# A graph-network kernel's prelude: the edge list on 124 partitions with four blocks each, places counted by two engines, ranks before most node tables, edge lists masked at their first use

## The chip, the cores and the metric

The kernel runs on one core of one Trainium2 chip. The metric is the device time of one execution in microseconds (us), the median of several runs; lower is better. A core has five engines that work through instruction queues of their own: TensorE (PE in the profile; its weight loads are PEld), VectorE (DVE), ScalarE (ACT), GpSimd (POOL) and SyncE (SP). Transfers are started from the queues of SP and ACT, and, where the addresses come out of a tile in on-chip memory, from POOL ("indirect" gathers and scatters).

## The reference

The reference is two layers of a graph transformer on 3125 nodes of 256 features, with 103125 directed edges sorted by their destination (`dst`), each with a source (`src`) and one of eight types.

```python
xn = _layernorm(x)
x = x + _L0_gnn_ref(xn, src, dst, ...) + _L0_mix_ref(xn, ...)     # max over the edges of a node
x = x + _L0_ffn_ref(_layernorm(x), ...)                          # experts chosen for the whole graph
xn = _layernorm(x)
x = x + _L1_gnn_ref(xn, src, dst, edge_type_8, ...) + _L1_mix_ref(xn, ...)   # sum over the edges of a node
x = x + _L1_ffn_ref(_layernorm(x), ...)                          # two of eight experts for each node
```

In layer 0 the graph part of node n is `relu(theta(x_n - x_s) + phi(x_s))`, maximised over all edges s to n. As the part of n is constant, the kernel maximises rows of a table `btab` = normalised x times (phi - theta), and adds the node's own part afterwards. In layer 1 it is a sum of rows picked from a table by source and type.

## The kernel before

**Layout.** 3125 nodes are 25 tiles of 128. Nearly all arithmetic is float32. The node tile t=24 has 53 real rows.

**The prelude** (lines 922 to 1230) turns the sorted edge list into a form in which one indirect gather brings one edge for each of 128 nodes:

1. *Places.* For each node its place `en` is needed, the number of edges whose destination is at most that node. It is found in two steps. `firsts` holds the first destination of each block of 128 edges (806 blocks), read by a transfer of single numbers into `blk0`, turned round by seven products on PE and copied by ACT (L1097, L1098). A quad is four tiles in which partition p holds nodes 4p to 4p+3; there are seven quads, the last with one tile. For each quad `counts_of` (DVE, L1057) or `signs_of` (ACT, L1050) counts the blocks that begin at or below the quad's first node, `stretches_of` fetches a stretch of 416 destinations for each partition from there (POOL, `row`), and `places_of` (DVE, L1076) counts in it for each of the quad's tiles. `at_i` is the place as an integer.
2. *Lists.* `edges_of` (POOL, `raw`) fetches for every node the 64 entries of the combined index `e_idx` (source times 8 plus type) that end at its place; those that belong to other nodes are to be masked. There are 25 such fetches.
3. *Degrees and ranks.* `dg` is the difference of neighbouring places. Nodes are ranked by falling degree, by a one-hot `hot` of 66 degree keys, products on PE (L1146), copies on ACT (L1147), a scan and a sum on DVE (L1178 to L1184). The result is `in_i`, the node that stands at each rank, made by 25 one-hot products (L1225, L1226).
4. *Tables.* `node_stats` (DVE) and `node_table` (ACT, PE) normalise x and make `btab`, five tiles at a time (`fives`). `ntab` holds for each node its x and its list: x is copied early by five transfers, `masks(g)` (DVE, L1160 to L1162, three operations a quad) replaces foreign entries by a padding index and writes the lists.
5. *Checks.* `bad` (L1169 to L1175) is a test of whether the edge list is sorted and has the loops that the fast form needs; a general form of the kernel exists for other inputs and isn't taken here.

**Layer 0** follows in `fast()`: `fetch` gathers `nrow`, the rows of `ntab` in order of rank (POOL, `ask`), and splits them into x and the indices `idx1`, `idx2` (DVE, L1497, L1502). Then `edge_pass` makes for tile t `STEPS[t]` gathers of 128 rows of `btab`, at most four in one buffer, maximised on DVE. Because ranks fall in degree, a tile needs only as many gathers as its largest node has edges (814 in all). Dense work (attention, experts) is interleaved with these from a list with costs. `outputs_out` copies a product into a spare buffer `y1` (`SECONDS` of them) until `outputs_b` adds it on DVE.

**What sets the order.** In the prelude the queues of DVE, POOL and PE follow the program text (`manual_schedule`); ACT's and SP's are arranged by a planner. The first two fetches of layer 0 stand outside such a region, so there the planner arranges DVE too. Each queue is worked through in order: an instruction that waits holds all behind it. Transfers use eight completion counters in turn, so each new transfer of SP or ACT first waits for the one eight before it.

Of the kernel before, what the change touches and what calls it, by code (L numbers as in the profile page):

```python
# [20 lines left out]
P = 128  # L21
# [28 lines left out]
STRETCH = 416  # L50
# [8 lines left out]
SECONDS = 6  # L59
# [19 lines left out]
def gps_kernel(ctx: ExitStack, tc: tile.TileContext, a, out):  # L79
# [13 lines left out]
    e_idx = dram.tile([EPAD // W + 2, W], I32, name="e_idx")  # L93

    ntab = dram.tile([NPAD, D + W], F32, name="ntab")
# [828 lines left out]
    in_i = keep.tile([P, NT], I32, name="in_i")  # L924
    with ExitStack() as prx:
# [6 lines left out]
        blk0 = pre.tile([P, 7], I32, name="blk0")  # L932
        V.memset(blk0, 1 << 20)
        d_rows = a["dst"][:EPAD, :].rearrange("(j k) o -> j (k o)", k=P)
        d_wide = a["dst"][:EPAD, :].rearrange("(j k) o -> j (k o)", k=STRETCH)
        with nc.allow_non_contiguous_dma(reason="the first destination of each block of edges"):
            S.dma_start(blk0[:, 0:6], d_rows[: 6 * P, 0:1].rearrange("(c j) o -> j (c o)", j=P))
            S.dma_start(blk0[: TE - 6 * P, 6:7], d_rows[6 * P :, 0:1])
        src_i = pre.tile([P, TE], I32, name="src_i")
        S.dma_start(src_i, a["src"].rearrange("(p t) o -> p (t o)", t=TE))  # L940
        typ_i = pre.tile([P, TE], I32, name="typ_i")
        S.dma_start(typ_i, a["typ"].rearrange("(p t) o -> p (t o)", t=TE))
        dst_i = pre.tile([P, TE], I32, name="dst_i")
        S.dma_start(dst_i, a["dst"][:EPAD, :].rearrange("(p t) o -> p (t o)", t=TE))
        nxt_i = pre.tile([P, TE], I32, name="nxt_i")
        S.dma_start(nxt_i, a["dst"][1 : EPAD + 1, :].rearrange("(p t) o -> p (t o)", t=TE))
# [3 lines left out]
        for s in fives:  # L950
            nc.sync.dma_start(
                ntab[P * s.start : P * s.stop, :D].rearrange("(t p) d -> p t d", p=P), x[:, s, :]
            )
# [14 lines left out]
        real = pre.tile([P, NT], F32, name="real")  # L968
        V.tensor_scalar(real, dval, float(NN), None, op0=ALU.is_lt)
        en = pre.tile([P, 29], F32, name="en")  # L970
        V.memset(en[:, 0:1], 0.0)
        rev = pre.tile([P, W], F32, name="rev")
# [113 lines left out]
        def edges_of(q):  # L1086
# [3 lines left out]
            for t in range(s.start, s.stop):  # L1090
                gather_at(raws[q][:, t - s.start, :], e_idx[:], at_i[:, t : t + 1])
# [21 lines left out]
        for q in range(7):  # L1113
            places_of(q)
            edges_of(q)
            if q in (1, 4):
                node_table(fives[q // 3])
# [1265 lines left out]
```

## Time and profile before

| | us |
|---|---|
| median of 3 runs | 2598.07 |
| lowest, highest | 2595.62, 2602.01 |
| the profiled execution | 2597.56 |
| its span from first to last instruction | 2595.8 |
| first `row` fetch, first `raw` fetch, first `nrow` gather (POOL) | 24.85, 34.15, 105.97 |
| first gather from `btab` | 110.51 |
| last gather of layer 0 begins | 1182.41 |
| mean granted TensorE clock | 0.826 of full |

The times of rows five to seven are from the start of the span. The page lists the instructions of each engine with busy time, idle time before them and what ended that idle time ("<-"; "issue" means nothing that the profile shows). The timeline shows single instructions in order. A mean clock below one means that TensorE is throttled for part of the time. In the 40 slices of the page each digit is a tenth of busy time in 64.9 us.

### The profile page before, as it was taken

To read this page: it belongs to the slowest core of one execution; us is meant where nothing else is said; L and a number is where in the kernel's file an instruction comes from. 1 tells how busy PE (TensorE), PEld (TensorE's weight loads), DVE (VectorE), ACT (ScalarE), POOL (GpSimd) and SP (SyncE) were. 2 spreads that over 40 slices of the span, in tenths; PEclk is the share of its full clock that TensorE was granted. 3 is DMA by queue.
4 is the path that set the end of the run, shared out by engine and by line. 5 is a ranking of instruction groups with operands and counts; after the bars stand their busy time and mean duration, and the time that the engine had idled before them with its cause. 6 is when DMAs were issued, how large, how long until landed. Compare 5 with 4: busy or idle time off the path is not lost.

```text
span 2595.8 us, 20939 instructions
## 1 busy us (share of the span) xinstructions
PE 1802.9 (69%) x6146; PEld 1077.6 (42%) x6146; DVE 1258.8 (48%) x3093; ACT 551.3 (21%) x1297; POOL 1765.7 (68%) x1850
## 2 busy tenths in 40 slices
PE   3546787305844524764898618498898989998998
PEld 2423444104522312442343406243343545666787
DVE  6744545337344343443663244544635454655552
ACT  3213321002210100121121302121212222322343
POOL 5277777777777777772443677777776777777761
PEclk9667888656966757876999758698999999999999
DMA  6333334334333333331577753333333333333330
GB/s 195 110 105 110 104 104 122 103 102 133 103 103 103 103 102 103 103 104 60 224 306 305 235 155 103 110 100 107 98 103 90 102 110 106 101 104 104 102 96 17
DMA packets 129367, 314.68 MB, mean 121 GB/s; under 512 B 39520, under 2 KB 64166, under 8 KB 122836
## 3 DMA queue, kind: packets, MB, share of 16 engines
q0 software_dynamic: 86784, 252.60, 32.6%
q1 hardware_dynamic: 36526, 56.36, 6.1%
q10 hardware_dynamic: 5926, 4.21, 0.6%
q8 instruction: 53, 0.87, 0.1%
q14 instruction: 78, 0.64, 0.1%
HBM read 246.35 MB, written 66.69 MB: 121 GB/s over the span
## 4 chain that ended last, share of the span: by engine, by line
PE 25%; POOL 9%; issue 8%; DVE 5%; DMA 4%; ACT 1%; POOLq 0%; DVEq 0%; ACTq 0%
POOL gt L181 9%; PE py L2179 8%; PE mm L2146 8%; PE mm L176 6%; DMA gt<-htab_f,idx2g 2%; DVE gt L1266 1%; DMA htab_f<-hs,id_i 1%; PE pt L2156 1%; PE mm L2115 1%; PE mm L2040 1%; DVE bnst L150 1%; DVE acc L1271 0%; DMA out_dram<-x,id_i 0%; DVE hT L2164 0%; ACT L2150 0%
## 5 line engine op out<-in xcount | busy, mean ns | idle before, releaser
L181 POOL DMA_INDIRECT gt<-htab_f,idx2g x814 | 799.1, 982 | 270.0 <-issue 219.3
L181 POOL DMA_INDIRECT gt<-btab,idx x814 | 796.5, 978 | 249.8 <-issue 222.1
L1266 DVE TENSOR_TENSOR gt<-gt 128x256 f32<-128x256 f32 (+1 forms) x831 | 445.0, 536 | 740.6 <-DMA gt<-btab,idx 477.9
L2179 PE MATMUL py<-hT,w 128*128 128x256 f32 (+4 forms) x1408 | 383.0, 429 | 43.7 <-DVE hT L2164 43.7
L2146 PE MATMUL mm<-xT,w 128*128 128x256 f32 (+4 forms) x1408 | 373.6, 417 | 12.6 <-DVE x L2046 10.2
L2179 PEld LDWEIGHTS py<-hT,w 128*128 128x128 f32 x1408 | 245.0, 201 | 176.7 <-issue 82.1
L2146 PEld LDWEIGHTS mm<-xT,w 128*128 128x128 f32 x1408 | 240.6, 197 | 137.7 <-issue 87.0
L2150 ACT ACTIVATE hT<-mm,b 128x256 f32<-128x256 f32 (+4 forms) x352 | 170.1, 495 | 404.6 <-PE mm L2146 400.4
L176 PE MATMUL pt<-w_own,xT 128*128 128x256 f32 x100 | 39.0, 523 | 260.2 <-DVE acc L1675 260.2
L2164 DVE TENSOR_TENSOR hT<-hT,pt 128x1024 f32<-128x1024 f32 (+4 forms) x88 | 117.4, 1334 | 163.0 <-PE pt L2156 163.0
L176 PE MATMUL mm<-w_rel,xT 128*128 128x512 f32 x400 | 183.5, 618 | 4.5 <-ACT xT L171 3.6
L1271 DVE TENSOR_TENSOR acc<-acc,gt 128x256 f32<-128x256 f32 x403 | 172.8, 429 | 13.9
L176 PEld LDWEIGHTS pt<-w_own,xT 128*128 128x128 f32 x100 | 23.9, 264 | 271.2 <-DVE acc L1675 265.2
L176 PEld LDWEIGHTS mm<-w_rel,xT 128*128 128x128 f32 x400 | 78.0, 198 | 102.2 <-issue 87.4
L1413 PE MATMUL mm<-xT,w 128*128 128x384 f32 (+2 forms) x320 | 95.3, 464 | 16.5 <-DMA w<-in_f_W_dram 16.5
L1692 PE MATMUL pmean<-ones,xt 128*128 128x1 f32 (+1 forms) x100 | 21.8, 322 | 119.7 <-DVE xt L159 119.6
L1682 ACT ACTIVATE rs<-rs 128x3 f32<-128x3 f32 (+2 forms) x11 | 2.2, 203 | 471.6 <-DVE rs L1681 471.6
L1442 PE MATMUL mm<-w,hT 128*128 128x256 f32 x400 | 93.0, 386 | 0.8 <-ACT hT L1434 0.8
L228 POOL DMA_INDIRECT htab_f<-hs,id_i x25 | 24.8, 992 | 96.8 <-DMA htab_f<-hs,id_i 25.4
L176 PE MATMUL mm<-w_qkv,xT 128*128 128x512 f32 (+1 forms) x200 | 85.9, 552 | 0.5 <-ACT xT L171 0.5
L1442 PEld LDWEIGHTS mm<-w,hT 128*128 128x128 f32 x400 | 74.1, 190 | 28.8 <-issue 18.2
L1413 PEld LDWEIGHTS mm<-xT,w 128*128 128x128 f32 x320 | 64.0, 222 | 47.2 <-DMA w<-in_f_W_dram 15.3
(394 smaller groups left out, 2141.5 us busy)
## 6 DMA issues: line engine op xcount, KB each, us to landing
here<-hs SPq DMA_DIRECT2D x25, 1024.0 KB, 3.9
gt<-btab,idx POOLq DMA_INDIRECT x814, 2.8
gt<-htab_f,idx2g POOLq DMA_INDIRECT x814, 2.8
w<-in_f_W_dram SPq DMA_DIRECT2D x20, 512.0 KB, 9.3
ntab<-x SPq DMA_DIRECT2D x5, 640.0 KB, 9.0
btab<-bs SPq DMA_DIRECT2D x5, 640.0 KB
otab<-xn SPq DMA_DIRECT2D x25, 128.0 KB, 1.7
acc<-otab SPq DMA_DIRECT2D x25, 128.0 KB, 2.0
```

The costliest lines, as they stand in the source:

```text
L150: V.bn_stats(out=st, in_=src)
L176: PE.matmul(ps, lhs[:, c, t * P : (t + 1) * P], w[:, c, :], start=start and c == 0, stop=stop and c == 1)
L181: G.indirect_dma_start(out=dst, out_offset=None, in_=table, in_offset=bass.IndirectOffsetOnAxis(ap=idx, axis=0))
L1266: V.tensor_tensor(gt[:, :h, :], gt[:, :h, :], gt[:, m - h : m, :], op=op)
L1271: V.tensor_tensor(acc, own(t) if i == 0 else acc, gt[:, 0, :], op=op)
L1413: PE.matmul(ph[:, :n], w1[:, i, c, f * P : (f + 1) * P], xT[:, c, at0 : at0 + n], start=(c == 0), stop=(c == 1),)
L1442: PE.matmul(py[:, i * D : (i + 1) * D], hTs[i][:, f, j * P : (j + 1) * P], w2[:, i, f, :], start=False, stop=(f == FC - 1), skip_group_che ...
L2040: PE.matmul(pa, ones_row, b_lu, start=False, stop=True)
L2146: PE.matmul(ph[:, :n], w1s[e][:, c, f * P : (f + 1) * P], xT[:, c, at0 : at0 + n], start=(c == 0), stop=(c == 1),)
L2150: S.activation(hT[:, f, :n], ph[:, :n], AF.Gelu, bias=b1[:, e, f : f + 1])
L2164: V.tensor_tensor(hT[:, :, :n], hT[:, :, :n], wb[:, None, :n].to_broadcast([P, FC, n]), op=ALU.mult)
L2179: PE.matmul(self.py[c][:, :n], w2s[e][:, f, c * P : (c + 1) * P], hT[:, f, :n], start=False, stop=(e == NX - 1 and f == FC - 1),)
```

## The change

- The four edge arrays are laid on 124 partitions of 832 edges. A partition holds four blocks of 208, so `firsts` has 496 entries and comes out of `dst_i` itself; `blk0` and its transfers go. A stretch is 496 destinations. `dst_i` is loaded first.
- The counts of blocks and the fetches of stretches stand first in DVE's text; the constants, the `bad` operations, the first statistics and the subtraction that makes `w_b` stand behind them. Three of the five copies of x into `ntab` are issued ahead of `e_idx`, two behind it.
- The places of quads 1, 3 and 5 are counted on ACT by the sign function (`place_signs_of`), 12 instructions; DVE only scales the result.
- `node_table(0)` follows quad 0; the other four tables follow the rank products, each with its `node_stats` directly ahead (`node_stats(1)` after quad 1).
- The lists are no longer masked in the prelude. `raw` has one more column with the degree, `ntab` has 321 columns for 320, and `fetch` masks: three DVE operations for one.
- `SECONDS` is 5 for 6.

```diff
-STRETCH = 416
+STRETCH = 496
+
+LP, LT, BLOCK = 124, 832, 208
...
-SECONDS = 6
+SECONDS = 5
...
-    e_idx = dram.tile([EPAD // W + 2, W], I32, name="e_idx")
-    ntab = dram.tile([NPAD, D + W], F32, name="ntab")
+    e_idx = dram.tile([EPAD // W + 2, W], F32, name="e_idx")
+    ntab = dram.tile([NPAD, D + W + 1], F32, name="ntab")
...
-        blk0 = pre.tile([P, 7], I32, name="blk0")
-        V.memset(blk0, 1 << 20)
...
+        def list_load(name, ap):
+            t = pre.tile([LP, LT], I32, name=name)
+            S.dma_start(t, ap.rearrange("(p t) o -> p (t o)", t=LT))
+            return t
+
+        dst_i = list_load("dst_i", a["dst"][:EPAD, :])
+        src_i = list_load("src_i", a["src"])
+        typ_i = list_load("typ_i", a["typ"])
+        nxt_i = list_load("nxt_i", a["dst"][1 : EPAD + 1, :])
...
+        def place_signs_of(q):
+
+            for t in range(QUADS[q].start, QUADS[q].stop):
+                S.activation(
+                    signs, stretches[q], AF.Sign, bias=half[:, t : t + 1], scale=-1.0,
+                    accum_out=in_blk[:, t : t + 1],
+                )
+
+        def places_of(q):
+            s = QUADS[q]
+            if q % 2:
+                V.tensor_scalar(in_blk[:, s], in_blk[:, s], 0.5, 0.5 * STRETCH, op0=ALU.mult, op1=ALU.add)
+            else:
+                for t in range(s.start, s.stop):
+                    V.tensor_scalar(
+                        junk, stretches[q], dval[:, t : t + 1], 0.0, op0=ALU.is_le, op1=ALU.add,
+                        accum_out=in_blk[:, t : t + 1],
+                    )
...
+        V.tensor_copy(blk_f, dst_i[:, ::BLOCK])
+        for j in range(LT // BLOCK):
+            pt = ps_tr.tile([P, 2, P], F32, name="pt")
+            PE.transpose(pt[:, 0, :LP], blk_f[:, j : j + 1].to_broadcast([LP, P]), ident[:LP, :LP])
+            S.copy(firsts[:, j * LP : (j + 1) * LP], pt[:, 0, :LP])
+        for q in (4, 5, 6):
+            signs_of(q)
+        for q in range(4):
+            counts_of(q)
+        stretches_of(slice(0, 4))
+        idx2 = pre.tile([LP, LT], F32, name="idx2")
+        V.scalar_tensor_tensor(idx2, src_i, float(NX), typ_i, op0=ALU.mult, op1=ALU.add)
+        nc.sync.dma_start(e_idx.rearrange("r w -> (r w)")[W : W + EPAD].rearrange("(p t) -> p t", t=LT), idx2)
+        V.tensor_scalar(blk_n[:, 4:], blk_n[:, 4:], 0.5, 0.5 * NB, op0=ALU.mult, op1=ALU.add)
+        stretches_of(slice(4, 7))
...
+        for q in (1, 3, 5):
+            place_signs_of(q)
+
...
         node_stats(fives[0])
-        V.tensor_copy(blk_f, blk0)
-        for j in range(7):
...
         V.tensor_tensor(w_b, w_b, th0, op=ALU.subtract)
...
         for q in range(7):
             places_of(q)
             edges_of(q)
-            if q in (1, 4):
-                node_table(fives[q // 3])
+            if q == 0:
+                node_table(fives[0])
+            if q == 1:
+                node_stats(fives[1])
...
+        node_table(fives[1])
         for g in (2, 3, 4):
             node_stats(fives[g])
-        node_table(fives[2])
-        node_table(fives[3])
-        last_rows = node_table(fives[4])
-
-        def masks(g):
...
+            last_rows = node_table(fives[g])
+
+
+        for g in range(7):
+            q = QUADS[g]
+            k = q.stop - q.start
+            V.tensor_copy(raws[g][:, :k, W], dg[:, q])
+            nc.sync.dma_start(ntab[P * q.start : P * q.stop, D:].rearrange("(p j) w -> p j w", j=k), raws[g][:, :k, :])
...
-                    V.tensor_copy(idx2[:, t, :], row[:, D + W - U :])
+
+                    has = l0w.tile([P, W], F32, name="has")
+                    edges = row[:, D : D + W]
+                    V.tensor_scalar(has, rev, row[:, D + W :], None, op0=ALU.is_lt)
+                    V.scalar_tensor_tensor(edges, edges, -float(PAD), has, op0=ALU.add, op1=ALU.mult)
+                    V.tensor_scalar(idx2[:, t, :], edges[:, W - U :], float(PAD), None, op0=ALU.add)
```

## The prediction, made before the changed kernel ran

> **What bounds the kernel now.** The page's fifth part and its slices show a kernel led by GpSimd's indirect gathers outside a dense middle.
>
> ```profile
> span 2595.8 us, 20939 instructions
> ...
> POOL 5277777777777777772443677777776777777761
> ...
> L181 POOL DMA_INDIRECT gt<-btab,idx x814 | 796.5, 978 | 249.8 <-issue 222.1
> ```
>
> See that the 814 gathers of the first layer cost 0.98 us each and that their idle time is "issue", about 0.3 apiece. Between 110 and 1183 us the waits view finds nothing else that holds POOL beyond 2.2 us: one gather each 1.25 us. So if the first gather starts X earlier, all that follows starts X earlier. The change lies almost wholly before that gather, which starts at 110.51, so I read the timeline from 0 to 112 us (columns: start, us, engine, line, operation, idle before and its releaser).
>
> ```profile
> 11.13 1.28 ACT L1000 ACT_TABLE_LOAD   x1 [11.13 <-DVE blk_f L1094]
> ...
> 18.09 0.69 DVE L1099 TENSOR_TENSOR w_b<-w_b,th 128x512 f32<-128x512 f32 x1 [7.13 <-DMA w_b<-in_ph_T_dram]
> ...
> 19.61 1.05 DVE L1057 TENSOR_SCALAR_CACHE_REDUCE junk<-firsts,dval 128x806 bf16<-128x806 f32 x1
> ...
> 24.85 1.12 POOL L223 DMA_INDIRECT row<-in_dst_dram,blk_i  x1 [21.41 <-DVE blk_i L1068]
> ...
> 33.71 0.17 DVE L1082 CAST at_i<-en 128x4 int32<-128x4 f32 x1
> ...
> 56.18 0.17 DVE L1124 TENSOR_TENSOR dg<-en,mm 128x6 f32<-128x6 f32 x1 [5.15 <-PE mm L1121]
> ...
> 75.99 3.59 DVE L1178 TENSOR_TENSOR_SCAN cum<-one_f,all__489 128x1650 f32<-128x1650 bf16 x1
> ...
> 93.63 0.39 PE L1216 MATMUL mm<-bad,ones 128*128 128x3 f32 x2 [4.56 <-DVE bad L1214]
> ...
> 105.97 0.95 POOL L181 DMA_INDIRECT nrow<-ntab,in_i  x1 [39.44 <-DVE id_i L1230]
> ...
> 110.85 0.19 DVE L1497 CAST idx2g<-nrow 128x46 int32<-128x46 f32 x1 [1.09 <-DMA nrow<-ntab,in_i]
> ```
>
> Three DVE waits set this stretch: 7.1 us until 18.09 (the weights sit ahead of the counts), 2.6 until 30.69 (the first row of destinations lands), 5.15 until 56.18 (PE is still in two node tables when the places are known). From 59.4 to 93.5 DVE is nearly full, and then PE: 25 one-hot products, 93.9 to 105.1. POOL stands still for 39 us before 105.97, so its 25 list fetches (34 to 66.5) have slack.
>
> **The change, step by step.** I follow the new order of the built program and put on it durations of rows above; times count from the span's start.
>
> *Start.* The 806 four-byte reads (`blk0`) go; the firsts come from the destination list, now loaded first. The load in that place (`src_i` before) has its last packet at 5.18. In the new order the weight load `w_b` is still ahead of all of ACT's work and waits for x's first piece. That piece is 640 packets; while four lists share the DMA engines the trace moves 100 to 110 of them per us, so it lands near 8.3, `w_b` issues at 8.75 (trace: 0.45 after a last packet), and the table load ends at 10.4 (before 12.4). Four copies instead of seven: firsts complete at 11.7 (before 15.3). `w_b`'s subtraction no longer stands before the counts: four counts of 496. L1057 takes 1.05 for 806 elements and L1076 0.65 for 416: 1.03 ns an element, hence 0.77 in start-to-start steps at 496. 11.9 + 3.1 + 0.9 (three small operations, hand-over) = first row fetch at 15.9, **9 us early**.
>
> *Given back.* DVE then has, ahead of the places: the combined index 1.0, four small ones 0.8, the constants moved behind it 3.3 (from 2.67 to 6.19 before), the seven operations on `bad` 6.1 (68.86 to 74.87 before, times 832/806), the first statistics 2.9, the subtraction 0.7: 15.6 to 30.4. Places of quad 0: 4 x 0.77 + 0.44 = 3.5, so `at_i` at 33.9. Before it was done at 33.88. The 9 us buy no earlier list fetch; they bought room for the 6 us of `bad`, which stood late. The list fetches end near 66 as before.
>
> *Counts on ACT.* Quads 1, 3, 5 leave DVE: 12 x 0.69 = 8.3 us, for 3 x 0.2. ACT pays 12 counts (L1050: 0.97 + 0.19, a step of 1.1 at 806, so 0.78 at 496). With rows landing 5.3 us after issue (the trace's 5.2 and 5.8), they run from 22.7 to 32.0; then comes a second table load. Here a rule speaks against the change: the Trainium skill, "ScalarE: Activation LUTs", section "What ACT_TABLE_LOAD costs", gives a switch 1.28 us plus 1.38 for a drain. The row is 1.28 and the next activation starts at 12.42, so no drain is seen. By the row the square root ends at 33.5; DVE asks for it at 34.0 and nothing waits. By the rule it ends at 34.9 and costs 0.9. I take the row, and 0.4 for the thin margin. Then DVE: quad 1 done 34.9, statistics 37.8, quads 2 to 6 (3.5, 0.65, 3.5, 0.65, 1.2) 47.3.
>
> *Ranks.* Only one node table stands ahead of them on PE (done near 44), so the 5.15 us wait goes: `dg` at 48.1, `hot` ends 51.4 (59.48 before): **8.1 us**, 7.7 after the margin.
>
> *Tables against DVE.* Now four tables follow. The new order puts each group's root in ACT's queue between tiles of the table before it, and the reciprocal waits there, ahead of the next group's statistics. ACT: one tile, eight rank copies (3.3, L1147), then tables at 6.0 per five tiles (from L1017's starts, 74.64 to 80.63) and 0.2 per root: the roots come at 58.5, 63.0, 68.3, and the scan, after seven small copies (1.0), at 69.6. From `hot` to scan: 18.2 us against 16.5, although 7.1 us of DVE work left it: **1.7 us lost**. Off the path: `btab` of the third table now queues on SP behind three list writes that wait for these copies (about 70); ACT may wait for its buffer near 76, PE ends its tables by 83, before it is wanted.
>
> *After the scan.* Masks of quads 1 and 2 (1.15 each) are gone from DVE's chain: **+2.3**; the other four lay inside PE's products, except 0.35 us (PE's wait at 96.2): **+0.3**. PE's last chain starts at about 85 instead of 93.6. The sum before the first row is 7.7 - 1.7 + 2.3 + 0.3 = 8.6.
>
> *First fetch.* A row now needs three operations for the lists in place of one. In the new order the mask of the second tile stands before the shift of the first tile's index, so the first gather waits for the second row's landing: 110.85 + two steps 0.4 + hand-over 0.3 = 111.5 against 110.51: **-1.0**.
>
> *Masks beside the gathers.* 25 x 2 more operations of 0.2 = 10 us of DVE spread over 400 us in which it is about half idle. The rule that speaks against it: "SBUF — State Buffer", section "Who interferes with whom": a two-port copy or `tensor_scalar` shuts GpSimd out of its port for the whole instruction. By it, with three such operations a tile for two, up to 25 x 0.2 = 5 us. The rows: around 126 us three casts and three shifts ran under gathers of 0.95, unstretched. I take 0.5, and keep 0 to 5. Fewer spare `y1` buffers (5 for 6): the third copy of a group needs the previous group's first add, earlier in DVE's order; nothing, at worst 1. Rows of 1284 bytes for 1280: no row here shows odd rows; the nearest is the same gather (3.2 to 3.6 us landing): 0, between -0.5 (no reason for more gain) and 2.
>
> Sum: 8.6 - 1.0 - 0.5 = **7.1 us faster**. On the profiled execution 2597.56 (1.8 us more than its span of 2595.8) that is 2590.5; on the median of the runs, 2598.07, it is **2591.0**, which I forecast.
>
> **Rivals.**
> - *ACT is quicker than I reckon* (firsts near 10, or tables not in the way of the roots). For: ACT's waits at the start are short. The 1.7 us come back, and up to 2 from the start are of use only if the places move too: 10 to 12 us, 2587. Against: every root stands behind tiles.
> - *The head's gain stays in the head.* If rows land late or ACT's counts run longer (integer input is not shown there), each us past the 0.5 margin comes off; also 5 us of blocked GpSimd. Gain 0 to 3: 2596.
> - *Slower: the reciprocal in front of quad 1.* DVE's reciprocal for the first table waits for a root behind all twelve sign counts; quad 1's places, all later list fetches and the ranks wait behind it. Row 1 is taken to land at 22.6. Each us after 23 is lost; from about 30 the 7 us are used up, and at 38 the kernel is 8 us slower: 2606. Against it: even under full DMA load the first two rows took 5.8 and 5.2 us; it needs 12.
> - *It does nothing*, because the gathers had slack at their start: POOL waits 39 us for `in_i`, so no.
>
> **How the numbers follow.** My sum 0.62, ACT quicker 0.15, gain stays in the head 0.15, slower 0.08. 0.3% is 7.8 us, about what a measurement here tells from no change. My sum, 7.1 give or take 3, lies on this edge: half of it (0.30) is beyond. Faster: 0.30 + 0.15 = 0.45; same: 0.32 + 0.15 = 0.47; slower: 0.08. The unknown costs (0.9 drain, 5 port, 2 odd rows, 1 buffers) reach from 2591 to 2598 at the slow end, the quick ACT to 2585 at the other: range 2585 to 2598.
>
> **What would show it.** First row fetch at 16 (not 25); `at_i` of quad 0 still near 34, no DVE wait for a row; the first reciprocal of `rs` unwaited; `hot` ending near 51; DVE waiting for ACT's roots 4 us, then 1, then 2, and the scan at 69 to 70; PE's `bad` product at 85; the first row gather at 97 to 98, the first `btab` gather 5.5 us after it (4.5 before); gathers still 0.98 us in the mean. Wrong it would be made by a reciprocal that waits several us near 34, or by gathers above 0.985 in the mean (6 us over 814).

## The result, and the profile after

The changed kernel takes 2604.74 us (median of 20 runs, 2596.62 to 2607.21), the kernel before 2596.91 on the same chip (20 runs). The medians are 7.8 us apart and the means 5.6, to which the ratio of 1.0021 answers, with a 95% interval of 1.0013 to 1.0030: slower by 0.2 to 0.3 per cent, which is small but clear of no change. The forecast was 2591.0, with a range of 2585 to 2598. The time lies outside this range, and on the other side of the time before.

The profiled execution took 2603.32 us. First the lines of its page that answer to those of before.

```profile
span 2601.6 us, 20970 instructions
...
POOL 3577777777777777772443777777776777777760
...
L183 POOL DMA_INDIRECT gt<-btab,idx x814 | 796.9, 979 | 251.6 <-issue 221.5
```

The gathers themselves are unchanged: 979 ns in the mean for 978, idle 251.6 us for 249.8. So the question is again where they start. The timeline of the changed kernel, from 12 to 112 us (start, us, engine, line, operation, and in brackets the idle time before and its releaser):

```profile
12.04 0.17 DVE L1076 CAST blk_f<-dst_i 124x4 f32<-124x4 int32 x1 [8.57 <-DMA dst_i<-in_dst_dram]
15.29 2.20 ACTq L147 DMA_DIRECT2D w_b<-in_ph_T_dram  x1
24.09 1.12 POOL L225 DMA_INDIRECT row<-in_dst_dram,blk_i  x1 [20.66 <-DVE blk_i L1040]
32.35 1.03 DVE L1127 TENSOR_TENSOR big<-dst_i,nxt_i 124x832 f32<-124x832 int32 x1 [3.25 <-DMA nxt_i<-in_dst_dram]
45.34 0.17 DVE L1065 CAST at_i<-en 128x4 int32<-128x4 f32 x1
52.45 0.94 POOL L225 DMA_INDIRECT raw<-e_idx,at_i  x1 [19.74 <-DVE en L1064]
59.34 0.17 DVE L1149 TENSOR_TENSOR dg<-en,mm 128x6 f32<-128x6 f32 x1 [0.83 <-PE mm L1146]
78.29 3.59 DVE L1185 TENSOR_TENSOR_SCAN cum<-one_f,all__436 128x1650 f32<-128x1650 bf16 x1
93.91 0.45 PE L1221 MATMUL mm<-bad,ones 128*128 128x3 f32 x2 [2.29 <-DVE bad L1219]
105.55 0.94 POOL L183 DMA_INDIRECT nrow<-ntab,in_i  x1 [16.54 <-DVE id_i L1233]
110.64 0.25 DVE L1503 TENSOR_SCALAR has<-rev,nrow 128x64 f32<-128x64 f32 x1 [0.87 <-DMA nrow<-ntab,in_i]
110.81 0.18 DVE L1512 TENSOR_SCALAR idx<-idx2g 128x46 int32<-128x46 int32 x1
111.83 0.96 POOL L183 DMA_INDIRECT gt<-btab,idx  x1 [3.90 <-ACT x L1513]
```

See three things. DVE waits 8.57 us for the destination list, and later 3.25 more for `nxt_i`: of these the forecast had only a wait to about 5 for the first and none for the second. The weights are issued at 15.29, behind the landing of x's first piece, which was put at 8.3. And from `dg` on, the kernel is about where it was before: 59.34 for 56.18, 78.29 for 75.99, 93.91 for 93.63. The new order did save work; what it saved was used up by a start that came later. The table sets this beside the forecast (us from the start of the span; two profiles of the changed kernel, the second from the experiments).

| | before | forecast | after | after, 2nd |
|---|---|---|---|---|
| first row fetch | 24.9 | 15.9 | 24.1 | 24.5 |
| `at_i` of quad 0 done | 33.9 | 33.9 | 45.5 | 45.9 |
| end of `hot` | 59.5 | 51.4 | 62.8 | 62.6 |
| scan | 76.0 | 69.6 | 78.3 | 81.0 |
| PE's product of `bad` | 93.6 | 85 | 93.9 | 96.7 |
| first row gather | 106.0 | 97 to 98 | 105.6 | 108.2 |
| first `btab` gather | 110.5 | 102.9 | 111.8 | 114.5 |

(102.9 is 110.5 less the sum of 8.6 before the first row and plus the 1.0 of the first fetch.)

**Behind the gathers.** The last gather of layer 1 starts at 2518.5 before and 2517.6 after, so the longer time of this profile arises after it: the last output leaves 69.8 us later before, 76.5 later after. From 2557 us on PE works without a pause. Its row for 2560 to 2570 us (columns: busy time and number of instructions of PE, PEld, DVE, ACT, POOL, then PE's granted clock, DMA share, GB/s), of the kernel before:

```profile
2560.00:2570.00 10.00, 10.00 (x84) 9.52 (x84) 1.55 (x3) 2.94 (x8) 0.00 (x0) 1.00 0.01 2
```

and of the changed kernel:

```profile
2560.00:2570.00 10.00, 10.00 (x48) 9.31 (x47) 0.81 (x2) 2.20 (x6) 0.00 (x0) 0.56 0.00 0
```

84 products against 48 in the same 10 us: the clock stood at one half for 10.2 us from 2558.5 on, in which PE does 5.1 us less than at full clock. This is taken up again below.

### The profile page after: what moved, and what is told of

Its sections match the earlier page's. It is cut to its first block, busy times and chain, and to the rows that moved or that the text cites. A ratio compares the mean times of both kernels' runs of the same rounds, so it can differ in the third digit from the quotient of the medians.

```text
span 2601.6 us, 20970 instructions
## 1 busy us (share of the span) xinstructions
PE 1792.2 (69%) x6143; PEld 1072.0 (41%) x6143; DVE 1262.6 (49%) x3108; ACT 561.0 (22%) x1319; POOL 1772.0 (68%) x1850
## 3 DMA queue, kind: packets, MB, share of 16 engines
q0 software_dynamic: 86784, 252.90, 32.9%
## 4 chain that ended last, share of the span: by engine, by line
PE 26%; POOL 9%; issue 8%; DVE 5%; DMA 4%; ACT 1%; DVEq 0%; POOLq 0%; ACTq 0%
POOL gt L183 9%; PE mm L2156 8%; PE py L2189 8%; PE mm L178 7%; DMA gt<-htab_f,idx2g 3%; DVE gt L1269 1%; PE pt L2166 1%; PE mm L2050 1%; PE mm L2125 1%; DVE bnst L152 1%; DMA htab_f<-hs,id_i 1%; DVE hT L2174 0%; DMA out_dram<-x,id_i 0%; DVE acc L1274 0%; DMA xn<-here,own_i 0%
## 5 line engine op out<-in xcount | busy, mean ns | idle before, releaser
L183 POOL DMA_INDIRECT gt<-btab,idx x814 | 796.9, 979 | 251.6 <-issue 221.5
L1445 PE MATMUL mm<-w,hT 128*128 128x256 f32 x400 | 93.0, 386 | 0.1
L1445 PEld LDWEIGHTS mm<-w,hT 128*128 128x128 f32 x400 | 74.1, 190 | 28.1 <-issue 18.2
L1416 PEld LDWEIGHTS mm<-xT,w 128*128 128x128 f32 x320 | 63.6, 219 | 46.3 <-DMA w<-in_f_W_dram 15.3
## 6 DMA issues: line engine op xcount, KB each, us to landing
ntab<-x SPq DMA_DIRECT2D x5, 640.0 KB, 10.2
```

Source lines behind the costliest of these rows:

```text
L183: G.indirect_dma_start(out=dst, out_offset=None, in_=table, in_offset=bass.IndirectOffsetOnAxis(ap=idx, axis=0))
L1416: PE.matmul(ph[:, :n], w1[:, i, c, f * P : (f + 1) * P], xT[:, c, at0 : at0 + n], start=(c == 0), stop=(c == 1),)
L1445: PE.matmul(py[:, i * D : (i + 1) * D], hTs[i][:, f, j * P : (j + 1) * P], w2[:, i, f, :], start=False, stop=(f == FC - 1), skip_group_che ...
```

## The experiments

**Theory.** The transfers of 124 partitions run on few of the sixteen DMA engines. So the lists land late, and with them what shares those engines: x's first piece, the weights, the combined list. **Rivals:** the new order of DVE and ACT is what holds the head; or the head does gain, and the stretch from the ranks to the gathers takes it back.

The Trainium skill, "DMA: Bandwidth & Descriptors", section "Why a DMA increments its semaphore by 16 and not by 1", has a rule for it: a transfer uses the largest number of engines up to 16 that divides the size of the slowest dimension on both sides. That is 16 for 128 rows, and 4 for 124. The prediction did not weigh it. The trace agrees: a list packet of 3328 bytes occupies its engine for 0.182 us in the mean, so the 496 packets of four lists are 5.6 us of work for sixteen engines and 22.6 for four; they are on the way from 1.8 to 31.6, x's packets between them. Except for 0.1 us no more than four of these packets are under way at once; before, and with the lists cut as below, it is up to sixteen. The two weight matrices queue behind them: of their 512 packets 384 have landed by 19.6, and the other 128, a quarter, come from 30.2 to 37.8, when the lists are nearly through.

Three of the five groups of runs met chips on which the kernel before takes 3101 to 3138 us and PE leads layer 0 (its 814 gathers take 1281 to 1332 us from first to last instead of 1071 to 1076). Their total times are no measure for gains of the gathers, and the changed kernel itself was not run there. Their heads up to `hot` can be read for versions in the changed order, since PE does little there; in the order of before PE holds `dg` longer (DVE waits 8.59 us for it in a profile of the kernel before on such a chip, 5.15 in the first profile). Each ratio below is to the kernel before on the same chip.

### Lists cut so that all engines carry them

```diff
-            S.dma_start(t, ap.rearrange("(p t) o -> p (t o)", t=LT))
+            rows = ap.rearrange("(p t) o -> p (t o)", t=LT)
+            S.dma_start(t[:112], rows[:112])
+            G.dma_start(t[112:], rows[112:])
...
+        nc.sync.dma_start(e_rows[:112], idx2[:112])
+        nc.sync.dma_start(e_rows[112:], idx2[112:])
```

First on a chip with slow PE:

> The changed kernel with its four list loads, and the write of the combined list, each cut in two: 112 partitions (ScalarE's queue as before, SP for the write) and the other 12 (GpSimd's queue; SP for the write). Nothing else moves. Theory 'transfers': a transfer of 124 partitions goes out over 4 of the 16 DMA engines, so the lists land late and hold x's first piece, the weights, ScalarE's first work and the counts. Then the destination list's cast starts near 5.5 to 6 (12.0 in the changed kernel), the first row fetch near 17 (24.1), the first list fetch near 36 (52.5), the one-hot tile ends near 55 (62.8), the first gather of btab starts at 105, give or take 1.5 (111.8), and the median of the runs falls by 6 to 7 us. Rival 'order': the new order of DVE and ScalarE holds the head, not the landing of lists; then the first gather stays within 1.5 us of 111.8. Rival 'the ranks hide it': the one-hot tile ends 7 us earlier but the first gather moves by less than 3.

The first row fetch came at 16.1, `hot` began at 52.9; two relatives of the changed kernel with whole lists, on the same chip, show 25.1 and 61.3 to 61.7 there. The first `btab` gather came at 118.9, not at 105; the relatives have 129.8 and 133.6. Ratio 0.9974 (0.9950 to 0.9998), though the medians are alike (3139.83 and 3138.35). Then, with the changed kernel itself beside it, on a chip where the gathers lead (kernel before: 2597.80):

> The changed kernel once more, as the measure for the three beside it on this chip. From its own profile: first row fetch 24.1, one-hot tile 60.9, first gather of btab 111.8 us after the start of the span; median of the runs 5 to 8 us above that of the kernel before, of which 1 to 2 us lie ahead of the last btab gather and the rest behind it.

> The changed kernel with its list loads and the write of the combined list cut in 112 and 12 partitions. Theory 'transfers': first row fetch near 16, one-hot tile near 53 (60.9), the ranks and products behind it take as long as in the changed kernel, so that the scan starts near 70.3 (78.3), PE's product of bad at 86 (93.9) and the first btab gather at 103.9 (111.8); the run is 7 to 8 us shorter than the changed kernel and 1 to 6 shorter than the kernel before. Rival 'the ranks hide it': the first btab gather at 109 or later.

The changed kernel took 2603.22, ratio 1.0020 (1.0012 to 1.0028). With cut lists it took 2589.61, ratio 0.9977 (0.9965 to 0.9990). The timeline with cut lists:

```profile
9.42 0.17 DVE L1078 CAST blk_f<-dst_i 124x4 f32<-124x4 int32 x1 [3.69 <-DMA dst_i<-in_dst_dram]
15.48 1.66 POOL L225 DMA_INDIRECT row<-in_dst_dram,blk_i  x1 [9.70 <-DVE blk_i L1042]
23.77 0.71 ACT L1050 ACTIVATE signs<-row,half 128x496 bf16<-128x496 int32 x1 [9.77 <-DMA row<-in_dst_dram,blk_i]
32.71 0.17 DVE L1067 CAST at_i<-en 128x4 int32<-128x4 f32 x1
35.29 0.19 DVE L977 RECIPROCAL rs<-rs 128x5 f32<-128x5 f32 x1 [2.41 <-ACT rs L973]
50.27 1.88 DVE L1165 TENSOR_TENSOR hot<-key,io_f 128x1650 bf16<-128x1650 f32 x1
67.65 3.58 DVE L1189 TENSOR_TENSOR_SCAN cum<-one_f,all__441 128x1650 f32<-128x1650 bf16 x1
83.31 0.58 PE L1225 MATMUL mm<-bad,ones 128*128 128x3 f32 x2 [2.77 <-DVE bad L1223]
95.09 0.94 POOL L183 DMA_INDIRECT nrow<-ntab,in_i  x1 [21.13 <-DVE id_i L1237]
101.73 0.96 POOL L183 DMA_INDIRECT gt<-btab,idx  x1 [4.25 <-DVE idx L1516]
```

Beside the forecast (15.9, 33.9, `hot` from 49.5 to 51.4, 69.6, 85, 97 to 98, 102.9), every mark lies within 2.9 us, most within 1.7. The gain that was forecast is there, and it hung on the landing of the lists. In part the agreement of the first mark is luck: the weights are issued at 6.6, 2.1 earlier than forecast, and the destination list is used at 9.4, not from 5.2 on; the two errors meet in the same 15.5. The edit also moves twelve rows of each list to GpSimd's queue, but this is not what helps, since these are the rows that come last. The share of the DMA engines at work from 20 to 24 us shows why, in the changed kernel:

```profile
20.00:24.00 4.00, 0.00 (x0) 0.00 (x0) 3.46 (x11) 2.50 (x7) 0.00 (x0) 1.00 0.34 123
```

and with cut lists:

```profile
20.00:24.00 4.00, 0.00 (x0) 0.00 (x0) 3.90 (x6) 0.23 (x1) 3.39 (x3) 1.00 1.07 372
```

A third of the engines' time and 123 GB/s, while SP stands over the next transfers (3.65 us from 18.70, 4.77 from 23.43); against full engines and 372 GB/s. Both rivals fall: with the same order the first `btab` gather is 10 to 13 us earlier than in the two profiles of the changed kernel, and the stretch between passes the gain on.

### The kernel before, with its lists on 124 partitions alone

```diff
-        src_i = pre.tile([P, TE], I32, name="src_i")
+        src_i = pre.tile([LP, LT], I32, name="src_i")
...
-        idx2 = pre.tile([P, TE], I32, name="idx2")
+        idx2 = pre.tile([LP, LT], I32, name="idx2")
```

> The kernel before with one part of the change alone: its four lists and the combined list on 124 partitions of 832 (the first destinations still come from the 806 four-byte reads, the order of all work is that of before). Theory 'transfers': the lists take the time of 4 engines, the weights land behind them on those engines near 36 (17.4 before), the subtraction of the weights stands in front of the counts on DVE, so the first row fetch starts near 43 (24.9), the first gather of btab near 127 (110.5), and the kernel is 13 to 20 us slower. Rival 'order': the layout costs nothing, the first gather is within 1.5 us of 110.5.

> The kernel before with its lists on 124 partitions alone. From the first look at it: the weights' subtraction waits for their landing until 35, the first row fetch starts at 42 (24.9). Theory 'transfers': here too, and since the order of before has the counts behind that subtraction, the ranks, the products and the gathers all start 14 to 20 us later: first btab gather at 125 to 131, median 13 to 20 us above the kernel before. Rival: the 5.2 us that DVE waits for PE in front of the ranks and the slack of the fetches take part of it; less than 10.

Both runs were on chips with slow PE. Ratios 1.0072 (1.0050 to 1.0094) and 1.0094 (1.0070 to 1.0117), or 22 and 19 us between the medians: on these chips this part alone costs more than the whole change does on the others. The timeline of the second run:

```profile
37.66 0.69 DVE L1100 TENSOR_TENSOR w_b<-w_b,th 128x512 f32<-128x512 f32 x1 [22.23 <-DMA w_b<-in_ph_T_dram]
44.45 1.12 POOL L224 DMA_INDIRECT row<-in_dst_dram,blk_i  x1 [41.02 <-DVE blk_i L1069]
98.52 0.17 DVE L1125 TENSOR_TENSOR dg<-en,mm 128x6 f32<-128x6 f32 x1 [22.18 <-PE mm L1122]
```

The weights, 128 rows that would use all engines, wait behind lists on a quarter of them: 22.23 us for 7.13 (20.30 in the first run). The row fetch is 20 and 17 us late; 18 were expected. The first `btab` gather came at 151.5 and 154.3, not at 127: PE's two tables, which start late as well, hold `dg` for 22.2 and 22.6 us (5.15 before). Part of that is the chip's slow PE: the kernel before on a third chip of that kind waits 8.59 there and has its first gather at 126.5. Against that one the lists alone cost 25 and 28 us.

### The first two rows one after the other

```diff
-            fetch(2)
+            with tc.manual_schedule(engines={mybir.EngineType.DVE}):
+                ask(2)
+                fetch(1)
+                fetch(2)
```

> The changed kernel with the first two node rows handled one after the other on DVE: the shift of the first tile's index stands before the mask of the second tile. Theory of the prediction's step 'first fetch': the first gather of btab starts 1.0 to 1.3 us earlier (110.5 to 110.8 for 111.8), its 6.3 us behind the first row gather fall to 5.0, and the end moves by as much. Rival: the gather waits for the copy within in_i as in the kernel before, whatever the order of DVE; then it starts at 110.5 at the earliest, but 0.3 or less earlier if that copy is itself late.

> As the one with cut transfers, and the first two node rows handled one after the other on DVE. First btab gather 5.0 to 5.5 us after the first row gather (6.3), so near 102.8; 1.0 us shorter than with cut transfers alone, 8 to 9 shorter than the changed kernel, 3 to 7 shorter than the kernel before. Rival: the index of the first tile isn't what its gather waits for (the copy within in_i is); then the distance stays at 6.0 to 6.3.

The first run (slow PE) has 5.5 us from row gather to `btab` gather, for 6.3; ratio 0.9991 (0.9962 to 1.0020), nothing that can be told from none. With cut lists, on the chip of those runs:

```profile
98.31 0.94 POOL L183 DMA_INDIRECT nrow<-ntab,in_i  x1 [27.44 <-DVE id_i L1237]
101.97 0.25 DVE L1507 TENSOR_SCALAR has<-rev,nrow 128x64 f32<-128x64 f32 x1 [3.84 <-DMA nrow<-ntab,in_i]
102.74 0.19 DVE L1516 TENSOR_SCALAR idx<-idx2g 128x46 int32<-128x46 int32 x1
103.76 0.96 POOL L183 DMA_INDIRECT gt<-btab,idx  x1 [3.07 <-SPq L2396]
```

5.45 us for 6.64 with cut lists alone. The distance shrinks as expected. The time does not: 2592.54, ratio 0.9984 (0.9976 to 0.9992), with a first gather 2.0 later than with cut lists alone, because in this profile the destination list landed 1.3 later and the way from `hot` to the scan was 1.5 longer. The step is right, and smaller than what varies from execution to execution.

### The masks back in the prelude

```diff
+        def masks(g):
...
+            V.tensor_tensor(has, rev[:, None, :].to_broadcast(sh), dg[:, q, None].to_broadcast(sh), op=ALU.is_lt)
+            V.scalar_tensor_tensor(edges, edges, -float(PAD), has, op0=ALU.add, op1=ALU.mult)
+            V.tensor_scalar(edges, edges, float(PAD), None, op0=ALU.add)
...
-                    V.tensor_scalar(has, rev, row[:, D + W :], None, op0=ALU.is_lt)
...
+                    V.tensor_copy(idx2[:, t, :], row[:, D + W - U : D + W])
```

> The changed kernel with the lists masked in the prelude as before (seven masks beside the ranks), one copy and one shift for each row fetched in the first layer, rows still 1284 bytes. The prediction's steps: PE's product of bad starts 2.3 us later (96.2 for 93.9), the first row gather 2.6 later (108.1), the first gather of btab follows it after 4.6 instead of 6.3, so near 112.8 (111.8), and over the 814 gathers 0.5 us come back: the median within 1 us of that of the changed kernel. Rival 'GpSimd is blocked by the masks beside the gathers': then 3 to 5 us come back by the last gather of btab, and the kernel is 2 to 4 us quicker than the changed one.

> The changed kernel with the lists masked in the prelude as before, on a chip on which layer 0 is led by the gathers. From the first look at it: two us more between the scan and PE's product of bad (17.7 for 15.7), 0.8 more for PE's 25 products, and 1.4 less between the first row gather and the first btab gather. Theory of the prediction (masks beside the gathers cost 0.5): median within 2 us of the changed kernel. Rival (GpSimd is shut out by the masks, 5 us): 2 to 4 us quicker than the changed kernel, and the stretch from the first to the last btab gather 4 to 5 us shorter than 1071 to 1072.6.

> The changed kernel with the lists masked in the prelude. By the step 'masks': 2.0 more ahead of PE's product, 0.8 more in PE's products, 1.4 less at the first fetch, so the first btab gather 1.4 later than the changed kernel's; 0.5 comes back beside the gathers; median 0 to 2 above the changed kernel's. Rival (GpSimd shut out by the masks' port): the stretch of the 814 gathers falls by 4 to 5 and the median by 2 to 4.

All three met slow PE; ratios 1.0026 (1.0005 to 1.0047), 0.9973 (0.9948 to 0.9997), 1.0013 (0.9982 to 1.0045), which don't agree. The head can be read: from scan to PE's product 17.7 us for 15.7, PE's products 11.7 for 10.9, from row gather to `btab` gather 4.8 to 4.9 for 6.3. So moving the masks is worth 2.0 + 0.8 less about 1.4 in the head. (In two of the three runs the row gather also stands 1.7 us behind `in_i` for 0.5, waiting for the last list writes, which come later when masks go ahead of them.) What the masks cost beside the gathers stays open: from first to last `btab` gather it is 1071.9 us in two profiles of the order of before and 1071.0 to 1076.0 in six with masks in the pass, which holds the 0.5 of the prediction and nearly the 5 that it took from the rule. The mean gather takes 0.977 to 0.983 us in these six, for 0.978 before.

### The roots out of the way of the tables

```diff
         for g in (2, 3, 4):
             node_stats(fives[g])
+        for g in (2, 3, 4):
             last_rows = node_table(fives[g])
```

> The changed kernel with the statistics of the last three groups of nodes put back ahead of their tables, as the kernel before has them; nothing else moves. The prediction's step 'tables against DVE' says that DVE's waits for ScalarE's roots (4.9 and 7.7 us in the two profiles of the changed kernel, nothing before) come from their place between the tables' tiles: then these waits go, the scan starts 12 to 14 us after the end of the one-hot tile (15.5 and 18.4), and PE, which waits 2.3 to 2.8 us for bad in the changed kernel, becomes the limit, so that the first btab gather starts 2 to 4 us earlier in relation to the one-hot tile (49 and 52 us behind its end in the changed kernel) and the median falls by 2 to 4. Rival: PE's tables end the stretch anyway; then the scan is earlier and the gather is not, by more than 1.

> The changed kernel with the statistics of the last three groups ahead of their tables, on a chip on which the gathers lead layer 0. The theory (DVE stands behind ScalarE's roots, and these behind PE's tiles): scan 12 to 14 us after the end of the one-hot tile, first btab gather 2 to 4 us earlier than in the changed kernel (111.8 and 114.5), median 2 to 4 below the changed kernel's, about that of the kernel before plus 2. Rival: PE's tables end the stretch: gather not earlier by more than 1.

> The changed kernel with the statistics ahead of the tables, once more for a chip on which the gathers lead layer 0. Theory: scan 12 to 14 us after the end of the one-hot tile, first btab gather at 109 to 111 (111.8 and 114.5), median 2 to 4 below the changed kernel. Rival: PE's tables end the stretch, the gather is not earlier by more than 1.

In the changed order DVE asks for a root that stands in ACT's queue between tiles of the table before it, and each of these tiles waits for PE. On the chips with slow PE this is dear. A relative of the changed kernel (rows one after the other; on another such chip the one with the masks back has 17.17):

```profile
89.88 0.19 DVE L975 RECIPROCAL rs<-rs 128x5 f32<-128x5 f32 x1 [16.95 <-ACT rs L971]
```

and the changed kernel with the statistics ahead, on that other chip:

```profile
73.78 0.19 DVE L975 RECIPROCAL rs<-rs 128x5 f32<-128x5 f32 x1 [2.10 <-ACT rs L971]
```

There it seems to pay: ratios 0.9952 (0.9925 to 0.9979) and 0.9975 (0.9953 to 0.9997), the first gather at 114.3 and 125.2, where relatives with whole lists have 129.8 to 134.4. Only the first of the two has the forecast scan, 12.4 us after `hot`; in the second it is 22.0, with a reciprocal that stands for 8.0 us with nothing recorded that it waits for. On the chip where the gathers lead (kernel before: 2602.17) it was the other way: 2614.76, ratio 1.0052 (1.0034 to 1.0070), first gather at 119.3. Neither the theory nor its rival expected that. The timeline of SP's queue in its profile, and ACT and DVE after it:

```profile
78.37 0.38 SPq L995 DMA_DIRECT2D btab<-bs  x1
78.96 14.26 SPq L1184 DMA_DIRECT2D ntab<-raw  x5
93.31 17.11 SPq L995 DMA_DIRECT2D btab<-bs  x3
...
96.77 0.37 ACT L983 COPY bs<-mm 128x256 f32<-128x256 f32 x1 [4.93 <-DMA btab<-bs]
...
103.38 0.16 DVE L1226 TENSOR_REDUCE bad<-mm 128x1 f32<-128x3 f32 x1 [11.44 <-PE mm L1222]
```

The scan does come 11.4 us after `hot`, for 15.5 and 18.4. But now the list writes are ready sooner and stand on SP ahead of the table writes. They wait for the last list fetch, issued at 89.5; the tables queue behind them, ACT waits 4.93 for the buffer of such a table, PE with it, and DVE 11.4 for PE. The fetches are late because the combined list, issued at 41 and written over four engines, lets them start at 54 only; but this is hardly later than in the changed kernel (52.5). PE's clock was also at one half for 17.1 us around the end of `hot` (10.2 and 13.7 in the two profiles of the changed kernel) and for 6.8 more just ahead of PE's product of `bad`; how the loss divides between the two wasn't tried apart.

### The three together

> Cut transfers, first two rows one after the other, and the statistics ahead of the tables. If the three act on different stretches they add: the first btab gather at 99 to 101.5 (103.8 with the first two), the median 2 to 4 us below that of the first two, 7 to 12 below the kernel before. Rival: the gains overlap, the gather at 103 or later.

> Cut transfers, rows one after the other, statistics ahead. If the three add: first btab gather at 99 to 101.5, median 9 to 13 us below that of the kernel before. Rival: PE's tables, which now end the stretch, eat the third; gather at 103, 6 to 8 below.

> The three together, for such a chip. If they add: first btab gather at 99 to 101.5, median 9 to 13 below the kernel before. Rival: PE's tables now end the stretch and eat the third; gather at 103, 6 to 8 below.

Slow PE: ratios 0.9928 (0.9901 to 0.9956) and 0.9975 (0.9951 to 0.9999), first gather at 116.6 and 114.2. Where the gathers lead: 2594.44 for 2602.17, ratio **0.9958** (0.9941 to 0.9974).

```profile
63.25 3.58 DVE L1190 TENSOR_TENSOR_SCAN cum<-one_f,all__441 128x1650 f32<-128x1650 bf16 x1
...
92.20 0.18 DVE L1237 TENSOR_SCALAR in_i<-mm 128x25 int32<-128x25 f32 x1 [1.30 <-PE mm L1234]
...
99.79 0.96 POOL L183 DMA_INDIRECT gt<-btab,idx  x1 [4.75 <-DVE idx2g L1510]
```

With lists that land in time, the statistics ahead help: first gather at 99.8, 4.0 earlier than with the first two. PE's product of `bad` is only 1.2 earlier, so PE's tables end that stretch, as the rival said (the same wait for the table's buffer, 3.9 us), but DVE has its one-hot tiles ready by then, and the 25 products take 6.9 us for 11.3. The median fell by 7.7, the mean by 10.1, with seven runs, so that these don't settle whether the 9 to 13 of the sum are reached. This version and the one with cut lists alone are both faster than the kernel before. The changed kernel is slower than that on both chips where it was timed. Which of them is better is not settled: they were not timed on the same chip.

### Later starts, and the end of the kernel

```diff
         V.tensor_copy(id_i, pi[:, :NT])
+        for _ in range(2):
+            V.memset(cum, 0.0)
+            V.tensor_copy(cum[:, 0:1], in_i[:, 0:1])
+        V.tensor_scalar(in_i, pi[:, :NT], float(NN - 1), None, op0=ALU.min)
```

> The kernel before with two fills of a dead tile and a repeated minimum between the node numbers and the first row gather: all of layer 0 and what follows starts later by that much (about 3 to 5 us, read off as the start of the first btab gather against 110.5), and nothing else changes. Theory 'the end of the kernel is PE at the clock that is granted there[...]': the middle of the runs moves by another amount than the delay, since the share of runs with a half-speed stretch in the last 80 us changes with it. Rival 'a start that is later by d ends later by d': the median moves by the delay, give or take 1.

> The kernel before, for a second profile beside the three below: the first btab gather near 109 to 111, the last output scatter about 70 us behind the last gather of layer 1 (69.8 in the first profile; 73 to 76 in those of the changed kernel and its relatives). If that last stretch is 73 or more here too, the longer end is no mark of the changed kernel.

The kernel before with this delay puts the first row gather 4.71 us behind `in_i` for 0.86, so 3.85 later; its median is 2602.0 for 2597.8, 4.2 more, ratio 1.0022 (1.0010 to 1.0033). This fits the rival, that a start later by d ends later by d, but it is weak: by the mark that was named for d, the first `btab` gather, the profile shows 2.6, since all ahead of the delay came early in it, and the interval of the ratio is 2.6 to 8.6 us. If it holds, the changed kernel's first gather, 1.3 and 4.0 later in its two profiles than in that of before, would account for that much of the 5.4 and 7.8 us between the medians. The profiles don't show it: in both the last gather of layer 1 starts 0.9 and 0.8 earlier than before. The second run, the kernel before against itself, met slow PE (first `btab` gather at 126.5, last output 82 us behind the last gather) and says nothing on the end (ratio 1.0013, 0.9989 to 1.0038: what such a chip can tell apart).

The end itself in the profiles of chips where the gathers lead: from the last gather to the gates of the last tiles (PE's L2136 or its like), from there to the last output, and the time that PE's clock stood at one half within this second part (the last 8 us of the record left out), in us:

| | to the gates | to the last output | at one half |
|---|---|---|---|
| before; before, delayed | 36.6; 36.2 | 33.1; 33.1 | 0; 0 |
| after | 38.5 | 37.9 | 10.2 |
| after, 2nd | 38.6 | 34.7 | 3.4 |
| cut lists; and rows in order | 39.8; 41.1 | 34.7; 34.7 | 3.4; 3.4 |
| statistics ahead | 36.2 | 33.1 | 0 |
| the three together | 38.5 | 34.7 | 3.4 |

Two things follow. The last part is PE's alone: 33.1 us at full clock, and half of each slow stretch on top (1.7 for 3.4, 5.1 for 10.2; measured 1.6 and 4.8). And the two versions whose gathers end earliest have the longest way to the gates (39.8 and 41.1), the one whose gathers end last has 36.2; so it seems that earlier gathers leave PE further behind and not all of their gain arrives. It is not the whole of it: the changed kernel's gathers end 0.9 earlier, and its way is 1.9 longer. In the first pair of profiles the changed kernel reaches the gates 1.0 us later than the kernel before, and loses 4.8 of its 5.8 us behind them.

Each such stretch begins 2.2 to 2.4 us after PE takes up work again behind a pause of 1.43 for the gates, which all eight profiles have. The Trainium skill, "TensorE: Matmul & The Clock Gate", section "What's actually happening", says that windows of 3413 ns that run freely set the clock, and that it falls to one half after a window without work. The record agrees in the step: every stretch at one clock but the last is a multiple of 3.41 us. It does not agree in the other: no window here is without work. The one ahead of the fall has 1.80 to 1.97 us of PE's work in the five profiles with such a stretch, while elsewhere in the changed kernel's first profile a window with 1.75 keeps the full clock and two in which PE is busy throughout, ending at 1882.7 and 2142.1, are followed by one half. So what lets the clock fall here is open, and how the windows lie to the pause may be chance. The version with statistics ahead has no such stretch, so it is no mark of the changed kernel; how often each kernel meets it, and so how the 5.4 and 7.8 us divide, the runs don't show.

## Why the prediction was wrong

**The step that failed is *Start*: it priced the landing of the new lists at the rate of the old ones.** For the destination list it took 5.18, the last packet of `src_i` before, a load of 128 rows. And it said that x's first piece "lands near 8.3, `w_b` issues at 8.75", because "while four lists share the DMA engines the trace moves 100 to 110 of them per us". That rate was that of transfers of 128 partitions. With 124 the destination list is used at 12.0, x's piece lets the weights go at 15.3, `nxt_i` holds DVE until 32.4, and the first row fetch is at 24.1 instead of 15.9. The places were to be done at 33.9 and were done at 45.5: 11.6 us, more than the whole gain, of which 8.2 are there at the row fetch and 3.25 are the wait for `nxt_i`. At the first `btab` gather 8.9 and 11.6 us are missing in the two profiles, of 13.7 between the forecast and the median. With the lists cut the same step measures 15.5 and 32.9, the first of these by two errors that cancel (above).

**All that follows starts X earlier** was the frame. It holds only roughly: from the first `btab` gather to the last gather of layer 1 the eight profiles of chips where the gathers lead have 2403 to 2415 us, and 69 to 76 from there to the last output. What the changed kernel loses against the one before lies in its profiles behind the last gather (1.9 and 2.0 to the gates; 4.8 and 1.6 behind them, at half clock); why its median is 5 to 8 us above stays open.

**Given back** was right: the 9 us at the start buy no earlier places, they make room for `bad` and the constants (with cut lists `at_i` is done at 32.9, 1.0 earlier).

**Counts on ACT.** No drain was seen: the second table load runs from 42.60 for 1.28, and the root starts at 43.89. The margin was too thin, though. With cut lists the rows are used 8.3 us after the fetch instead of 5.3, and DVE waits 2.4 us for the root in front of quad 1. This is the mechanism of the prediction's slower rival, at a small size. In the changed kernel itself that reciprocal waits for nothing, since all of DVE was late.

**Ranks.** The wait of 5.15 for PE went (0.83 is left). 8.1 us were forecast for the end of `hot`; with cut lists 7.3 are measured (52.2 for 59.5), in the changed kernel it is 3.3 later than before.

**Tables against DVE.** 18.2 us from `hot` to scan were forecast; 15.5 and 18.4 were measured, 15.5 and 17.0 with cut lists, 16.5 before. The mechanism is as described. The size goes with PE's clock, which the step took as one value: PE is at half clock for 4.0 and 11.0 us of this stretch in the two profiles of the changed kernel and for 3.3 and 8.1 with cut lists, and the waits for roots add up to 4.9, 7.7, 4.9 and 6.3. The remark that table writes on SP would queue behind list writes was also right; it was put off the path, and it comes onto it as soon as the tables move up.

**After the scan** 2.3 were forecast for the masks; 2.0 and 0.8 in PE's products were measured. **First fetch:** 1.0 forecast for the order, 0.8 to 1.2 measured for it alone; from row gather to `btab` gather it is 6.3 for 4.5, 1.7 in all. **Masks beside the gathers:** open between -1 and 4.

The sum was thus nearly right for a kernel whose lists arrive in time: 7.1 us forecast, 8.2 measured between the medians (2589.61 and 2597.80), 6.0 by the ratio.

## What to carry to other kernels

The number of rows of a transfer decided here on how many engines it ran (128 and 112 on sixteen, 124 on four), so a new layout is priced by its own row count before the rate of the old one is used; the badly split transfers also delayed others on the same engines. When work is moved ahead in one queue, look at what stands behind it in the queues that it touches: here roots behind tiles, and table writes behind list writes. A gain at the start is found in the total only as far as each stage behind it hands it on, so read the marks stage by stage, over more than one execution.

## What the runs showed that was not expected

- 124 rows against 112 and 12: 123 GB/s against 372 between 20 and 24 us, the weights landing at 37.8 against 15.7.
- The same program takes 2597 to 2602 us on some chips and 3101 to 3138 on others. On the latter PE stands still for 10 us and more at a time with nothing recorded that it waits for (10.5 ahead of one of the experts' products in layer 0, L1445; for the kernel before such stops ahead of these products, L1442, add up to 128 us in a profile of such a chip and to none where the gathers lead), while its granted clock is one half or full in the record. What holds it there is open.
- A fetch's small part on GpSimd's queue (39 KB, 12 rows) takes 7.0 us to land while the other queues are full, so with cut lists the destination list is used at 9.4, not at 5.5 to 6 as was expected. ACT's first copy of `firsts` then waits 1.9 us for it, so this small part is what sets the start of that version.
